# A cross attention's sums over the values kept in one PSUM bank for a whole group of heads, with seven banks in turn and two buffers for an unused output

## The chip, the core and the metric

The kernel runs on one core of a Trainium2 chip. The metric is the device time of one execution in microseconds; the kernel before took 2520.08 (the median of 3 runs, 2517.69 to 2526.74). The engines are named as in the profile: PE is TensorE's matmuls, PEld its weight loads, DVE is VectorE, ACT is ScalarE, POOL is GpSimd and SP is the engine whose queue issues most DMAs.

## What is computed

A small Perceiver network of four layers: 128 rows of width 256 (x) attend to 12544 rows of context, with self attention and feed-forward parts between. Each layer adds three blocks to x: a cross attention (xattn), an attention (attn) and a feed-forward (ffn). The change touches the second cross attention alone:

```python
def _L1_xattn_ref(K_in, V_in, Q_in, mask_attn, mask_pad, Wk, bk, Wv, bv, Wq, bq, Wo, bo):
    # D = 256, NH = 16 heads, DK = 16
    K = (K_in @ Wk + bk).reshape(b, l, NH, DK).transpose(0, 2, 1, 3)
    V = (V_in @ Wv + bv).reshape(b, l, NH, DK).transpose(0, 2, 1, 3)
    Q = (Q_in @ Wq + bq).reshape(b, lp, NH, DK).transpose(0, 2, 1, 3)
    KQ = jnp.einsum('bhld,bhpd->bhlp', K, Q) / np.float32(np.sqrt(DK))
    KQ = KQ + mask_pad.reshape(b, 1, l, 1)
    KQ = KQ + mask_attn.T.reshape(1, 1, l, lp)
    alpha = jax.nn.softmax(KQ, axis=2)
    O = jnp.einsum('bhlp,bhld->bhpd', alpha, V)
    O = O.transpose(0, 2, 1, 3).reshape(b, lp, NH * DK)
    return O @ Wo + bo
```

Here l is 12544, lp is 128, and mask_attn is a matrix of 128 x 12544 that is added to the scores of every head.

## The kernel before

**Stages.** The twelve blocks run one after the other (`run`, L1301). All four cross attentions are one function, `cross` (L361); the second is called as "l1x" with `side=True` (L1317). `side` means that the score has a matrix to be added, which is read from memory in two orders: as it is (`ft`, fetched in `fetch_k`, L441 to 444) and transposed (`gt`, in `fetch_v`, L459 to 464).

**Projections as jobs.** The keys and values of all four cross attentions (`project`, L192) stand in one list of small jobs: a job projects 512 keys (`keys`, L204) or 256 rows of values (`values` of `project`, L220), has ACT or DVE copy the result out of PSUM, and writes it to memory from POOL's queue. `pump` (L142) takes the next jobs of the list. Cross attentions and other blocks pump jobs between their own steps, so a stage also does the projections of later stages. In `cross` a stage's own jobs are due by `goal` (L630 to 633), and others by `rate`, a number per step for each phase: 0.95, 0, 1.2, 1.2 and 0.4 for l1x.

**Steps of cross.** The 12544 context rows are cut into NST = 25 tiles of 512 (the last has 256). The 16 heads are cut into 4 groups (`units`) of 4 (`width`). A step of the loop (L619) handles two things: the scores whose maxima are needed for tile `km`, and, `lead` = 27 steps later, the scores that are exponentiated for tile `ke`. So the first 27 steps have maxima only, the next 73 both, the last 27 only exponentials; at 25 steps a group of heads ends. All is under `manual_schedule` (L616): every engine takes its instructions in the order in which the loop writes them.

Within a step (`scores`, L550), with both:
- set 1: s products of heads 2 and 3, t products of heads 0 and 1, on PE; then their drains;
- set 2: s products of heads 0 and 1, t products of heads 2 and 3; then their drains;
- the jobs that are due (L633, L637);
- `values` (L573): the sums over the values for the tile `ke` of the step before.

An s product (`score_s`, L471) is a matrix of 128 queries x 512 keys in a bank of PSUM. Its drain, with `side`, is one `tensor_tensor_reduce` on DVE (L492): it adds `ft`, takes the maximum into a column of `mxs`, and writes the sum to a tile "junk" that nobody reads; "junk" has one buffer. In the profile it is two instructions, CUSTOM_DVE_ANT_0 and DVE_READ_ACCUMULATOR2_ANT. A t product (`score_t`, L519) is 512 keys x 128 queries in a bank; DVE adds `gt` into the tile `e` (L542) and ACT takes the exponential in place (L547).

`values` multiplies the exponentials with the values (32 matmuls on PE as the profile counts them, tile p, L589) into one bank, and DVE adds that bank to a tile `acc` in SBUF (L595), or copies it there at a group's first tile (L593). After the group `finish` (L597) divides by the sum of the exponentials.

**Banks.** PSUM has eight banks. `bank` (L134) gives out one tile of a whole bank at a time, in turn: bank 1, 2, ... 7, 0. Every user calls it: each head's s and t product, each job, `lower` (L511), `finish` and `values`. A tile of a bank waits until the last reader of the tile that held the bank before is done. PE takes its instructions in order, so a matmul that waits for its bank holds up all that is behind it.

**Loads.** SP's queue issues the loads of keys, values, `ft`, `gt` and context in the loop's order; a load into a buffer that is still being read waits at the head of that queue.

Of the kernel before, what the change touches and what calls it, by code (L numbers as in the profile page):

```python
# [10 lines left out]
F32 = mybir.dt.float32  # L11
# [7 lines left out]
P = 128  # L19
# [6 lines left out]
NST = -(-S2 // ST)  # L26
# [43 lines left out]
def _gelu_kinks():  # L70

    at = [0.25 * i for i in range(17)]
    even = [0.5 * a * math.erf(a / math.sqrt(2.0)) for a in at]
    slope = [(even[i + 1] - even[i]) / 0.25 for i in range(16)]
    return [(at[i], slope[i] - (slope[i - 1] if i else 0.0)) for i in range(16)]


class Net:
    def __init__(self, ctx, tc, io):
        self.tc, self.nc, self.io = tc, tc.nc, io  # L80
        nc = self.nc
        cp = ctx.enter_context(tc.tile_pool(name="const", bufs=1))
        self.small = ctx.enter_context(tc.tile_pool(name="small", bufs=2))
        self.xp = ctx.enter_context(tc.tile_pool(name="x", bufs=2))
        self.wp = ctx.enter_context(tc.tile_pool(name="w", bufs=3))
        self.bp = ctx.enter_context(tc.tile_pool(name="bg", bufs=2))
        self.dp = ctx.enter_context(tc.tile_pool(name="scratch", bufs=1, space=DRAM))
        self.ps1 = ctx.enter_context(tc.tile_pool(name="ps1", bufs=1, space=PSUM))

        self.x = self.xp.tile([P, D], F32, name="x0", tag="x")  # L90
        nc.sync.dma_start(out=self.x, in_=io["x"])
        self.cst = cp.tile([P, NCONST], F32, name="cst", tag="cst")
        nc.sync.dma_start(out=self.cst, in_=io["cst"])
        self.cols = cp.tile([P, NCOL], F32, name="cols", tag="cols")
        nc.scalar.dma_start(out=self.cols, in_=io["cols"])
        self.rows = cp.tile([P, NROW], F32, name="rows", tag="rows")
        nc.gpsimd.dma_start(out=self.rows, in_=io["rows"].to_broadcast([P, NROW]))
        self.eps = {}
        for e in (EPS, 1e-6):
            t = cp.tile([P, 1], F32, name=f"eps{len(self.eps)}", tag=f"eps{len(self.eps)}")  # L100
            nc.vector.memset(t, e)
            self.eps[e] = t
        self.ident = self.const("ident")
        self.kinks = cp.tile([P, 16], F32, name="kinks", tag="kinks")
        for i, (at, _) in enumerate(_gelu_kinks()):
            nc.gpsimd.memset(self.kinks[:, i : i + 1], -at)
        self.fold = cp.tile([P, 64], F32, name="fold", tag="fold")
        nc.gpsimd.tensor_tensor(out=self.fold, in0=self.ident[:, 0:64], in1=self.ident[:, 64:128],
                                op=ALU.add)

        self.plan, self.tiles, self.loaded = [], {}, 0
        self.jobs, self.share, self.credit, self.side = [], 0.0, 0.0, False
        self.turn, self.done = 0, set()

    def const(self, name):
        at, n = CONST_AT[name]
# [17 lines left out]

    def bank(self, name):

        self.turn = (self.turn + 1) % 8
        return self.ps1.tile([P, 512], F32, name=name, tag=f"bank{self.turn}")


# [220 lines left out]
    def cross(self, name, side=False, project=True, rate=()):  # L361
# [2 lines left out]


        nc, tc = self.nc, self.tc
        self.share, self.side = 0.0, side
        width = WIDTH[name]
        units = 16 // width
        lead = NST + 2  # L370
# [2 lines left out]
        with ExitStack() as es:  # L373
# [13 lines left out]
            ps = self.bank(f"{name}_q")  # L387
# [17 lines left out]
            kt, vt, ft, gt, mxs, es_, acc = {}, {}, {}, {}, {}, {}, {}  # L405
# [60 lines left out]
            def tile_of(u, j):  # L466

                at = 32 * ((width * u + j) % 4)
                return slice(at, at + 32)

            def score_s(k, heads):  # L471

                u, i = divmod(k, NST)
                s, m = i * ST, min(ST, S2 - i * ST)
                if u not in mxs:
                    mxs[u] = pool.tile([P, width, NST], F32, name=f"{name}_mxs{u}", tag="mxs",
                                       bufs=2)
                t, at = kt[u, s // SB], s % SB
                banks = {j: self.bank(f"{name}_s{k}_{j}") for j in heads}

                def products():
                    for j in heads:
                        r = tile_of(u, j)
                        nc.tensor.matmul(banks[j][:, :m], qb[u][r, :], t[r, at : at + m],  # L484
                                         start=True, stop=True)

                def drain():
                    for j in heads:
                        if side:
                            junk = ep.tile([P, ST], F32, name=f"{name}_j{k}_{j}", tag="junk",  # L490
                                           bufs=1)
                            nc.vector.tensor_tensor_reduce(  # L492
                                out=junk[:, :m], in0=banks[j][:, :m], in1=ft[k][:, :m], scale=1.0,
                                scalar=-3.0e38, op0=ALU.add, op1=ALU.max,
                                accum_out=mxs[u][:, j, i : i + 1])
                        else:
                            nc.vector.tensor_reduce(out=mxs[u][:, j, i : i + 1],  # L497
                                                    in_=banks[j][:, :m], axis=AX.X, op=ALU.max)
                return products, drain
# [73 lines left out]
            def values(ks):  # L573


                u, i = divmod(ks[0], NST)
                ps = self.bank(f"{name}_p{ks[0]}")
                todo = []
                for k in ks:
                    s = (k - u * NST) * ST  # L580
                    m = min(ST, S2 - s)
                    v, at, e = vt[u, s // SB], (s % SB) // P, es_.pop(k)
                    for a in range(m // P):
                        for j in range(width):
                            c = 17 * (width * (at + a) + j)
                            todo.append(((width * a + j) % 4, v[:, c : c + 32],
                                         e[:, j, a * P : (a + 1) * P]))
                for n, (c, lhs, rhs) in enumerate(todo):
                    nc.tensor.matmul(ps[32 * c : 32 * c + 32, :P], lhs, rhs, start=n < 4,  # L589
                                     stop=n >= len(todo) - 4, skip_group_check=True)  # L590
                if i == 0:
                    acc[u] = self.small.tile([P, P], F32, name=f"{name}_at{u}", tag="at")
                    nc.vector.tensor_copy(acc[u], ps[:, :P])  # L593
                else:
                    nc.vector.tensor_tensor(out=acc[u], in0=acc[u], in1=ps[:, :P], op=ALU.add)  # L595
# [20 lines left out]
            with tc.manual_schedule():  # L616
                for k in (0, 1):
                    fetch_k(k)
                for at in range(total + lead + 3):  # L619
# [21 lines left out]
                    while waiting:  # L641
                        u, i = divmod(waiting[0], NST)
                        n = NST - i if NST - i < 2 * batch else batch
                        last = waiting[0] + n - 1
                        if ke is not None and ke - last < behind - batch + 1:
                            break
                        if last > waiting[-1]:
                            break
                        values(waiting[:n])
                        waiting = waiting[n:]  # L650
                    if ke is not None:
                        waiting.append(ke)
                    u, i = divmod(at - lead - 2 - NST, NST)
# [1 line left out]
                        finish(u)  # L655

            nc.vector.tensor_tensor(out=o, in0=o, in1=self.row(f"{name}_vb"), op=ALU.add)
            self.share, self.side = 1.0, False
            if not project:
                self.add_to_x([o], name)  # L660
                return
# [1 line left out]
            ps = self.one(f"{name}_pr")  # L663
# [720 lines left out]
def _device_arrays(I):  # L1384
# [15 lines left out]
    def cross(name, q, k, v, o=None):  # L1400
        a[f"w_{name}"] = cat(*(_padded(q.T).T,) if o is None else (_padded(q.T).T, o))
        a[f"w_{name}_kv"] = cat(k, v)

    cross("l0x", I["L0_xattn_q_w"].T, I["L0_xattn_k_w"].T, I["L0_xattn_v_w"].T)
    cross("l1x", *(I[f"L1_xattn_W{k}"] for k in "qkvo"))
    cross("l2x", *(I[f"L2_xattn_w{k}"] for k in "qkvo"))
    cross("l3x", *(I[f"L3_xattn_W{k}"] for k in "qkvo"))
    a["w_l0a"] = cat(I["L0_attn_Wq"].T, I["L0_attn_Wk"].T, I["L0_attn_Wv"].T)
# [73 lines left out]
```

## Time and profile before

| | us |
|---|---|
| median of 3 runs | 2520.08 |
| the profiled execution, its own time | 2514.97 |
| its span, first to last instruction | 2513.2 |
| second cross attention, first normalisation to the last sum | about 682 to 1345 |
| PE / DVE / ACT busy between 682 and 1345 | 649.72 / 535.87 / 317.67 |
| L492, the maxima of l1x, x400, busy on DVE | 271.1 |
| L542, the additions of l1x, x400, busy on DVE | 249.9 |
| L595, the additions to `acc`, x96, median of one | 0.280 |
| L593, the copies to `acc`, x4, median of one | 0.290 |

A group's mean is over the full tiles and the shorter last ones. Busy time of PE counts a matmul until its modelled end, and a matmul that stands before a waiting one can be counted as busy while it waits, so starts say more than busy shares. In a line of the timeline the columns are the start, the length, the engine, the line of the kernel, the operation, the output and the inputs; "x8" are eight merged instructions; a bracket gives idle time just before and what ended it.

### The profile page before, as it was taken

Reading aid. Unit: us, or ns where it says so; the run is one execution under the profiler, and the core shown is the slowest. Engines: PE = TensorE matmul, PEld = TensorE weight load, DVE = VectorE, ACT = ScalarE, POOL = GpSimd, SP = SyncE. Lnnn points to the kernel's source line nnn. Section 1 sums busy time; section 2 is a strip of 40 time slices with the busy share of each in tenths; the row PEclk is TensorE's granted clock in tenths of the full one; section 3 lists DMA queues with packets and bytes.
Section 4 is the critical chain, followed back from the end, with each engine's and each line's share of the span. In section 5 each row is a group of like instructions: output and inputs, shape, how many; then the busy total and the mean of one; then the engine's idle time right before and its main releaser. Section 6 shows DMA issues by size and latency. Waiting matters only on the chain.

```text
span 2513.2 us, 76921 instructions
## 1 busy us (share of the span) xinstructions
PE 2344.3 (93%) x32103; PEld 1722.2 (69%) x32103; DVE 1627.1 (65%) x3503; ACT 1144.7 (46%) x2109; POOL 637.6 (25%) x1297
## 2 busy tenths in 40 slices
PE   6989999997899999999999978899999949999969
PEld 3348888874536886666778734468888836888848
DVE  2446688722186788888887721598883579888431
ACT  1212356772213444545584134226668321666842
POOL 6874100015562112444301244630000112000001
PEclk9989999998999999999999989899999978999979
DMA  7768653227788887877665646663332633333216
GB/s 252 217 209 273 200 151 93 78 73 230 255 244 277 275 254 220 241 225 232 215 219 203 197 144 197 194 206 95 91 100 59 211 118 113 94 95 99 65 48 220
DMA packets 200504, 438.90 MB, mean 175 GB/s; under 512 B 33292, under 2 KB 90848, under 8 KB 196064
## 3 DMA queue, kind: packets, MB, share of 16 engines
q1 hardware_dynamic: 148208, 271.33, 35.8%
q0 software_dynamic: 51584, 161.42, 20.0%
q8 instruction: 255, 4.18, 0.7%
q10 hardware_dynamic: 368, 1.25, 0.1%
q14 instruction: 89, 0.73, 0.1%
HBM read 327.69 MB, written 112.58 MB: 175 GB/s over the span
## 4 chain that ended last, share of the span: by engine, by line
PE 33%; issue 14%; DVE 3%; DMA 2%; ACT 1%; POOL 0%; SPq 0%; ACTq 0%; DVEq 0%; POOLq 0%
PE l3x_t L534 5%; PE l3x_p L589 4%; PE l3x_s L484 4%; PE l2x_v L321 3%; PE l3x_k L321 3%; PE l3x_v L321 3%; PE l1x_t L534 2%; PE l1x_p L589 1%; PE l2x_s L484 1%; PE l1f_h L321 1%; PE l1f_o L321 1%; ACT l1x_e L547 1%; PE l2x_k L321 1%; PE l3f_h L321 1%; PE l3f_o L321 1%
## 5 line engine op out<-in xcount | busy, mean ns | idle before, releaser
L547 ACT ACTIVATE l1x_e<-l1x_e 128x512 f32<-128x512 f32 (+1 forms) x400 | 240.6, 622 | 245.9 <-DVE l1x_e L542 245.9
L492 DVE CUSTOM_DVE_ANT_0 l1x_j<-l1x_s,l1x_f 128x512 f32<-128x512 f32 (+1 forms) x400 | 271.1, 678 | 80.6 <-PE l1x_t L534 30.0
L497 DVE TENSOR_REDUCE l0x_mxs<-l0x_s 128x1 f32<-128x512 f32 (+1 forms) x400 | 244.4, 672 | 120.4 <-PE l0x_s L484 89.3
L547 ACT ACTIVATE l0x_e<-l0x_t 128x512 f32<-128x512 f32 (+1 forms) x400 | 203.4, 595 | 176.4 <-PE l0x_t L534 172.9
L547 ACT ACTIVATE l3x_e<-l3x_t 128x512 f32<-128x512 f32 (+1 forms) x400 | 203.4, 595 | 155.6 <-PE l3x_t L534 152.0
L497 DVE TENSOR_REDUCE l2x_mxs<-l2x_s 128x1 f32<-128x512 f32 (+1 forms) x400 | 243.5, 671 | 29.5 <-PE l2x_t L534 23.9
L497 DVE TENSOR_REDUCE l3x_mxs<-l3x_s 128x1 f32<-128x512 f32 (+1 forms) x400 | 242.8, 670 | 27.0 <-PE l3x_t L534 23.9
L547 ACT ACTIVATE l2x_e<-l2x_t 128x512 f32<-128x512 f32 (+1 forms) x400 | 203.5, 595 | 119.4 <-PE l2x_t L534 115.8
L542 DVE TENSOR_TENSOR l1x_e<-l1x_t,l1x_g 128x512 f32<-128x512 f32 (+1 forms) x400 | 249.9, 671 | 11.4 <-PE l1x_t L534 9.1
L534 PE MATMUL l1x_t<-l1x_qb,l1x_kt 32*128 32x128 f32 x3136 | 202.9, 283 | 2.8 <-ACT l1x_vs L238 0.6
L484 PE MATMUL l0x_s<-l0x_kt,l0x_qb 32*128 32x512 f32 (+1 forms) x800 | 190.9, 618 | 15.1 <-ACT l0x_ks L213 9.5
L484 PE MATMUL l1x_s<-l1x_kt,l1x_qb 32*128 32x512 f32 (+1 forms) x800 | 204.2, 616 | 0.6 <-issue 0.5
L484 PE MATMUL l3x_s<-l3x_kt,l3x_qb 32*128 32x512 f32 (+1 forms) x800 | 199.2, 655 | 0.5 <-issue 0.5
L534 PEld LDWEIGHTS l1x_t<-l1x_qb,l1x_kt 32*128 32x128 f32 x3136 | 170.4, 186 | 37.9 <-ACT l2x_ks L213 19.9
L484 PE MATMUL l2x_s<-l2x_kt,l2x_qb 32*128 32x512 f32 (+1 forms) x800 | 184.9, 611 | 0.5 <-issue 0.5
L534 PE MATMUL l3x_t<-l3x_qb,l3x_kt 32*128 32x128 f32 x3136 | 180.5, 280 | 0.1
L534 PE MATMUL l2x_t<-l2x_qb,l2x_kt 32*128 32x128 f32 x3136 | 180.2, 280 | 0.0
L534 PE MATMUL l0x_t<-l0x_qb,l0x_kt 32*128 32x128 f32 x3136 | 179.7, 280 | 0.4 <-DVE l0x_vs L240 0.3
L217 POOL DMA_DIRECT2D l1x_kx<-l1x_ks x208 | 99.5, 486 | 298.9 <-ACT l1x_ks L213 268.1
L534 PEld LDWEIGHTS l3x_t<-l3x_qb,l3x_kt 32*128 32x128 f32 x3136 | 160.3, 186 | 6.8 <-issue 5.0
L534 PEld LDWEIGHTS l0x_t<-l0x_qb,l0x_kt 32*128 32x128 f32 x3136 | 159.4, 186 | 7.3 <-issue 5.0
L534 PEld LDWEIGHTS l2x_t<-l2x_qb,l2x_kt 32*128 32x128 f32 x3136 | 159.9, 186 | 6.2 <-issue 5.0
(606 smaller groups left out, 4050.5 us busy)
## 6 DMA issues: line engine op xcount, KB each, us to landing
l1x_f<-in_fside SPq DMA_DIRECT2D x96, 256.0 KB
l1x_g<-in_fsideT SPq DMA_DIRECT2D x96, 256.0 KB
w<-in_w_l3f POOLq DMA_DIRECT2D x16, 1024.0 KB, 5.1
l0x_kt<-l0x_kx SPq DMA_DIRECT2D x192, 72.0 KB
l1x_kt<-l1x_kx SPq DMA_DIRECT2D x192, 72.0 KB
l2x_kt<-l2x_kx SPq DMA_DIRECT2D x192, 72.0 KB
l3x_kt<-l3x_kx SPq DMA_DIRECT2D x192, 72.0 KB
l0x_vx<-l0x_vs POOLq DMA_DIRECT2D x24, 544.0 KB, 6.6
```

The lines of the kernel that those rows point to most:

```text
L217: nc.gpsimd.dma_start(out=kx[8 * half + h, 2:18, :], in_=t["k"][16 * h : 16 * h + 16, :n])
L321: self.nc.tensor.matmul(out, a, b, start=(i == 0), stop=(i == len(lhs) - 1))
L484: nc.tensor.matmul(banks[j][:, :m], qb[u][r, :], t[r, at : at + m], start=True, stop=True)
L492: nc.vector.tensor_tensor_reduce(out=junk[:, :m], in0=banks[j][:, :m], in1=ft[k][:, :m], scale=1.0, scalar=-3.0e38, op0=ALU.add, op1=ALU.m ...
L497: nc.vector.tensor_reduce(out=mxs[u][:, j, i : i + 1], in_=banks[j][:, :m], axis=AX.X, op=ALU.max)
L534: nc.tensor.matmul(banks[j][:, a * P : (a + 1) * P], t[r, at + a * P : at + (a + 1) * P], qb[u][r, :], start=True, stop=True)
L542: nc.vector.tensor_tensor(out=e[:, j, :m], in0=src, in1=gt[k][:, : m // P, :].rearrange("p a q -> p (a q)"), op=ALU.add)
L547: nc.scalar.activation(e[:, j, :m], src, AF.Exp)
L589: nc.tensor.matmul(ps[32 * c : 32 * c + 32, :P], lhs, rhs, start=n < 4, stop=n >= len(todo) - 4, skip_group_check=True)
```

## The change

For the calls with `side`, which is l1x alone, three things change. `values` no longer takes a bank of the rotation: a group of four heads has one tile of bank 7 for all of its 25 tiles of 512 rows, the matmuls of the later tiles add to what is there, and the bank is copied to `acc` once, after the group's last tile. The rotation goes over seven banks (0 to 6) from the start of the call to its end, and over eight again after it. And "junk" has two buffers. The diff, cut to its core:

```diff
-        self.turn, self.done = 0, set()
+        self.turn, self.ring, self.done = 0, 8, set()
...
     def bank(self, name):

-        self.turn = (self.turn + 1) % 8
+        self.turn = (self.turn + 1) % self.ring
         return self.ps1.tile([P, 512], F32, name=name, tag=f"bank{self.turn}")
...
-        self.share, self.side = 0.0, side
+        self.share, self.side, self.ring = 0.0, side, 7 if side else 8
...
                             junk = ep.tile([P, ST], F32, name=f"{name}_j{k}_{j}", tag="junk",
-                                           bufs=1)
+                                           bufs=2)
...
                 u, i = divmod(ks[0], NST)
-                ps = self.bank(f"{name}_p{ks[0]}")
+                if not side:
+                    ps = self.bank(f"{name}_p{ks[0]}")
+                elif i == 0:
+                    ps = self.ps1.tile([P, 512], F32, name=f"{name}_p{u}", tag="bank7")
+                    acc[u] = ps
+                else:
+                    ps = acc[u]
...
                 for n, (c, lhs, rhs) in enumerate(todo):
-                    nc.tensor.matmul(ps[32 * c : 32 * c + 32, :P], lhs, rhs, start=n < 4,
-                                     stop=n >= len(todo) - 4, skip_group_check=True)
-                if i == 0:
+                    nc.tensor.matmul(ps[32 * c : 32 * c + 32, :P], lhs, rhs,
+                                     start=n < 4 and (i == 0 or not side),
+                                     stop=n >= len(todo) - 4 and (ks[-1] == NST * (u + 1) - 1 or not side),
+                                     skip_group_check=True)
+                if side:
+                    if ks[-1] == NST * (u + 1) - 1:
+                        acc[u] = self.small.tile([P, P], F32, name=f"{name}_at{u}", tag="at")
+                        nc.vector.tensor_copy(acc[u], ps[:, :P])
+                elif i == 0:
                     acc[u] = self.small.tile([P, P], F32, name=f"{name}_at{u}", tag="at")
                     nc.vector.tensor_copy(acc[u], ps[:, :P])
                 else:
...
-            self.share, self.side = 1.0, False
+            self.share, self.side, self.ring = 1.0, False, 8
```

## The prediction

> **What bounds the kernel now.** I first read the engines' shares on the page, then the table of windows over the second attention (cross "l1x", the only one with side=True, so the only code that the change touches), then the timelines of TensorE (PE) and VectorE (DVE) inside it.
>
> ```profile
> PE 2344.3 (93%) x32103; PEld 1722.2 (69%) x32103; DVE 1627.1 (65%) x3503; ACT 1144.7 (46%) x2109; POOL 637.6 (25%) x1297
> ...
> 689.00:751.00 62.00, 61.71 (x220) 24.02 (x220) 49.98 (x145) 10.78 (x16) 43.18 (x83) 1.00 0.81 245
> ...
> 806.50:918.40 111.90, 111.90 (x1416) 94.11 (x1412) 86.27 (x208) 53.83 (x96) 15.46 (x32) 1.00 0.85 270
> 918.40:954.00 35.60, 34.99 (x504) 26.31 (x500) 32.80 (x88) 16.01 (x28) 3.78 (x7) 1.00 0.75 225
> 954.00:1253.00 299.00, 297.42 (x3678) 193.35 (x3678) 254.48 (x639) 149.63 (x252) 113.27 (x237) 0.99 0.76 230
> ```
>
> Columns: window, its length, then busy time of PE, PEld, DVE, ACT and POOL, the granted clock, DMA share, GB/s. PE looks full everywhere, but its ends are modelled, so who waits must be read from starts. DVE is at 81% in the first stretch (only maxima) and 92% in 918 to 954.
>
> ```profile
> 700.41 0.69 DVE L492 CUSTOM_DVE_ANT_0 l1x_j<-l1x_s,l1x_f 128x512 f32<-128x512 f32 x1
> 701.03 0.08 DVE L492 DVE_READ_ACCUMULATOR2_ANT l1x_mxs<- 128x1 f32 x1
> 701.26 0.69 DVE L492 CUSTOM_DVE_ANT_0 l1x_j<-l1x_s,l1x_f 128x512 f32<-128x512 f32 x1
> ...
> 928.50 0.69 DVE L492 CUSTOM_DVE_ANT_0 l1x_j<-l1x_s,l1x_f 128x512 f32<-128x512 f32 x1
> 929.12 0.08 DVE L492 DVE_READ_ACCUMULATOR2_ANT l1x_mxs<- 128x1 f32 x1
> 929.12 1.28 DVE L542 TENSOR_TENSOR l1x_e<-l1x_t,l1x_g 128x512 f32<-128x512 f32 x2
> 930.32 0.28 DVE L595 TENSOR_TENSOR l1x_at<-l1x_at,l1x_p 128x128 f32<-128x128 f32 x1
> 930.51 0.68 DVE L492 CUSTOM_DVE_ANT_0 l1x_j<-l1x_s,l1x_f 128x512 f32<-128x512 f32 x1
> ```
>
> Two things are to be seen. A maximum is followed by the next maximum after 0.84 or 0.85 us, but by an addition after 0.62: the second maximum writes the same "junk" tile and starts 0.14 after the first's accumulator read ends, the addition does not. And the sum l1x_at (L595) takes DVE 0.19 to 0.20 (930.32 to 930.51) in every step. A step in which DVE never idles is 5.50 (925.02 to 930.52 or so, repeated).
>
> Where PE is the slower one, steps of one kind alternate:
>
> ```profile
> 806.52 0.70 PE L484 MATMUL l1x_s<-l1x_kt,l1x_qb 32*128 32x512 f32 x2
> ...
> 807.60 0.61 PE L534 MATMUL l1x_t<-l1x_qb,l1x_kt 32*128 32x128 f32 x8
> ...
> 808.49 3.72 PE L321 MATMUL l1x_v<-l1x_kvw,l1x_cv 128*128 128x256 f32 x16
> 812.14 1.08 PE L589 MATMUL l1x_p<-l1x_e,l1x_vt 128*32 128x128 f32 x32
> 813.15 0.70 PE L484 MATMUL l1x_s<-l1x_kt,l1x_qb 32*128 32x512 f32 x2
> ...
> 814.31 0.69 DVE L492 CUSTOM_DVE_ANT_0 l1x_j<-l1x_s,l1x_f 128x512 f32<-128x512 f32 x1 [0.73 <-PE l1x_t L534]
> 814.93 0.08 DVE L492 DVE_READ_ACCUMULATOR2_ANT l1x_mxs<- 128x1 f32 x1
> ```
>
> The step from 806.52 lasts 6.63: first set 1.01, second set 0.96, two projections 3.65, values 1.01. The second set's t products begin 1.08 after the step. The next step (813.15 to 820.50) lasts 7.35, because its t products had to wait for their bank until 1.60. DVE's first maximum starts 1.16 after the step's start, as soon as its score is there.
>
> **Bank waits, by counting.** A step takes banks in the order s2 s3 t0 t1 | s0 s1 t2 t3 | projections (n of them) | p. With eight banks a tile waits for the one eight places back; before, t2 so waits for the last projection of the step before (or t3 where n is 0), and t3 for the p of the step before. The waits agree:
>
> ```profile
> PEld l1x_t L534 <- ACT l2x_ks L213: 19.9, 30, 0.9
> ```
>
> After, p leaves the rotation, and the ring is seven. Counting seven back, every tile of a step up to t2 waits for the same predecessor as before (n = 0, 1 and 2). Three differ: t3 now waits for **s2 of the same step**, the first projection for s3 and the second for t0 of the same step.
>
> **The change part by part.**
>
> 1. Sums in PSUM. It removes 96 additions (L595) of 0.20 on DVE. The 4 copies (L593, 0.29) move to a group's end, where a group's next p, a step later, waits for them: DVE has done them by then, so zero; uncovered it would be 4 x 0.3 = 1.2 us. The matmuls are the same. Their own bank wait goes: on PE, p starts at the end of the projections already (812.14 is 808.49 + 3.65), so nothing is won there.
>
> 2. Two junk tiles. Each maximum that follows a maximum starts 0.22 to 0.23 earlier (0.84 becomes 0.61). A full step on DVE falls from 5.50 by 0.20 + 2 x 0.22 to 4.86; a step of four maxima alone from 3.36 to some 2.5.
>
> 3. Seven banks. Where DVE waits for PE at a step's start, the first maximum ends at 1.16 + 0.70, and the semaphore reaches PE 0.06 later (at 930.40 an addition ended, at 930.46 PE went on). So t3 cannot start before 1.92, in every step that has both products. In order behind it on PE: the rest of the set, projections, p, the next step. From a late t3 to the end of the set it took 1.07 (t3 free at 930.66, p at 931.73); the projections start at 2.99, against 1.97 in an unhindered step and 2.69 (820.50 less 4.66) in the hindered one. From there to the step's end the rows show 2.93 for n = 1 (1228.97: 2.57 to 5.50) and 4.66 for n = 2. So a step becomes 5.92 (n = 1) and 7.65 (n = 2). DVE's 4.86 fits inside, and DVE meanwhile has three other drains, so it does not starve. If the part of t2 issued earlier shortens the tail to 0.88 (814.96 to 815.84), they are 5.73 and 7.46.
>
> **The sum, stretch by stretch.**
> - 689 to 751, maxima alone: 18 steps of 3.36 on DVE. PE's floor is 2.99 (718.20 to 721.19: four scores and one projection of keys). 18 x 0.37 = 6.7, less the 1.5 of two stalls there that are not DVE's: -5.2 at most. DMA at 81% would go to some 90%; I take -5. The 5.5 us wait for a context block at 751 and the PE-bound steps to 806 stay.
> - 806.5 to 918.4: 16 steps with n = 2, 111.8 in all, 6.99 each. 16 x 7.65 = 122.4: **+10.6** (+7.5 with the short tail).
> - 918.4 to 954: one step n = 1 that goes from 4.91 to 5.92, then six without projections, which DVE bounds: five to six times 0.64 less, the first lost to the longer step: -2.5.
> - 954 to 1253: 31 steps n = 1 outside the group changes, 181.0 in all, become 31 x 5.92 = 183.5: +2.5. Eight steps n = 2, 7.30 on average, become 7.65: +2.8. (Short tail: -3.4 and +1.3.) The steps at the two group changes are taken as they are.
> - 1253 to 1345, no maxima: the chain there is t, four additions, four exponentials, p; the sum comes after the additions and hides behind PE, so 0 (at best -1 or -2).
>
> Total: -5 + 10.6 - 2.5 + 2.5 + 2.8 = **+8.4 us**; bounds -2 and +15. On the profiled span of 2513.2 (2514.97 with what lies around it) that is 2521.6. The profiled run lies 5 below the median of 2520.08; put on the median the forecast is 2528, +0.3%, which is within 0.5% (12.6 us), about what a measurement of this kernel can tell from no change.
>
> [...]
>
> **Rivals.**
> - **A, the wait is hidden (faster).** If t3's new predecessor does not hold PE up (another order of banks than I counted, or s2 drained earlier), what remains is DVE's relief. n = 1 steps go to 4.9 (1.97 + 2.93): 31 x 4.9 - 181 = -29; n = 2 to 6.63: -5.7 in the third stretch and 8 x 0.6 = -5 later; with -5 and -2.5 this is -47: 2473. For it: DVE is at 85% in 954 to 1253 and the waits for ACT there come from DVE being late. Against: the same counting gives before's waits. Chance 0.16, most of it with a part of that gain, about 2500.
> - **B, the pause between maxima is not the tile's (slower).** If it belongs to the accumulator read that each maximum ends with, the second buffer wins nothing: the first stretch stays, the fourth gives back 1 instead of 2.5, and the sum is 10.6 + 5.3 - 1 = +15 to +16: 2536. It decides as soon as a maximum after a maximum still takes over 0.8. For it: only maxima carry that read. Against: the addition after the read does not pause. Chance 0.20.
> - **C, DMA bounds the first stretch (slower).** 81% and 245 GB/s now; 751 to 760 shows 96% at 299. If each step still takes 3.3, the sum is +13.4: 2533. Chance 0.10.
> - **Forecast** 0.54: of it 0.42 within 0.5%, 0.12 above (its bound of +15 lies over 12.6).
>
> So faster 0.16, same 0.42, slower 0.20 + 0.10 + 0.12 = 0.42. The forecast's own range is 2518 to 2535. The range for 8 in 10 takes in B and C with the medians' spread (2517.69 to 2526.74), and A's milder part: 2508 to 2542.
>
> **What will show it.** Maxima 0.61 apart in the first stretch, its steps near 3.0 (else B or C). In 806 to 918, equal steps of about 7.5 to 7.65 in place of 6.63 and 7.35, with PEld l1x_t waiting for DVE l1x_mxs from 1.1 to 1.9 after each step's start; if that wait is absent or the steps are 6.63, A. Steps near 4.9 at 930. No L595 rows, four copies at the groups' ends. A wait of p for a copy of over 1 us, or a stall at the start of the next stage, would be something I have not counted.

## The result, and the profile after

The changed kernel takes 2516.97 us (median of 12 runs, 2503.3 to 2527.15), the kernel before 2518.24 in the 12 runs beside them. The ratio is 1.0002, 95% interval 0.9984 to 1.002: no change that can be measured. The profiled execution of the changed kernel has a span of 2515.0 against 2513.2. The second attention alone, from its first score to its last sum over values, went from 651.5 to 649.9 us in the two profiles.

That the total stands still hides much movement. First the busy time of the changed kernel's engines:

```profile
PE 2347.4 (93%) x32103; PEld 1723.6 (69%) x32103; DVE 1586.1 (63%) x3407; ACT 1144.3 (45%) x2109; POOL 638.6 (25%) x1297
```

DVE has 96 instructions and 41 us less, PE is nearly as it was. The windows of the second attention, in the columns used above:

```profile
688.00:742.00 54.00, 53.38 (x204) 19.96 (x203) 41.48 (x132) 10.03 (x15) 34.82 (x68) 0.94 0.83 257
...
797.30:919.90 122.60, 122.60 (x1417) 95.03 (x1410) 78.86 (x192) 54.77 (x97) 15.50 (x32) 1.00 0.79 249
919.90:953.20 33.30, 32.72 (x502) 25.09 (x499) 31.04 (x82) 15.96 (x28) 3.79 (x7) 1.00 0.79 235
953.20:1251.40 298.20, 298.00 (x3681) 198.22 (x3677) 236.82 (x593) 149.63 (x253) 113.38 (x237) 1.00 0.76 230
```

The stretch with two projections per step was 111.9 long and is 122.6; PE counts as busy through all of it, in both. Where the time went is seen in the starts. PE's timeline of one such step:

```profile
805.01 0.70 PE L484 MATMUL l1x_s<-l1x_kt,l1x_qb 32*128 32x512 f32 x2
805.03 0.71 PE L534 MATMUL l1x_t<-l1x_qb,l1x_kt 32*128 32x128 f32 x8
805.55 0.59 PE L484 MATMUL l1x_s<-l1x_kt,l1x_qb 32*128 32x512 f32 x2
805.58 0.67 PE L534 MATMUL l1x_t<-l1x_qb,l1x_kt 32*128 32x128 f32 x9
806.02 0.60 PE L484 MATMUL l1x_s<-l1x_kt,l1x_qb 32*128 32x512 f32 x2
806.09 0.27 PE L534 MATMUL l1x_t<-l1x_qb,l1x_kt 32*128 32x128 f32 x1
806.46 0.59 PE L484 MATMUL l1x_s<-l1x_kt,l1x_qb 32*128 32x512 f32 x2
806.93 1.15 PE L534 MATMUL l1x_t<-l1x_qb,l1x_kt 32*128 32x128 f32 x14
808.01 3.72 PE L321 MATMUL l1x_v<-l1x_kvw,l1x_cv 128*128 128x256 f32 x16
811.66 1.08 PE L595 MATMUL l1x_p<-l1x_e,l1x_vt 128*32 128x128 f32 x32
812.67 0.70 PE L484 MATMUL l1x_s<-l1x_kt,l1x_qb 32*128 32x512 f32 x2
```

Of the second set's 16 t matmuls two go by 806.09, both of t2; the other 14 wait until 806.93, which is 1.92 after the step's start, and the step lasts 7.66. All 16 steps of the stretch are alike; the alternation of 6.63 and 7.35 is gone. DVE in the same step, then PEld's waits for t products in this stretch (total, times, longest), first in the changed kernel, then in the kernel before:

```profile
806.17 0.69 DVE L492 CUSTOM_DVE_ANT_0 l1x_j<-l1x_s,l1x_f 128x512 f32<-128x512 f32 x1 [2.73 <-PE l1x_t L534]
806.79 0.08 DVE L492 DVE_READ_ACCUMULATOR2_ANT l1x_mxs<- 128x1 f32 x1
806.79 0.69 DVE L492 CUSTOM_DVE_ANT_0 l1x_j<-l1x_s,l1x_f 128x512 f32<-128x512 f32 x1
```

```profile
PEld l1x_t L534 <- DVE l1x_mxs L492: 11.3, 16, 0.7
...
PEld l1x_t L534 <- ACT l1x_vs L238: 1.6, 8, 0.2
```

The first maximum's read ends at 806.87, and PE goes on at 806.93. Sixteen such waits in sixteen steps; before, PEld l1x_t waited here eight times for ACT's copy of a projection and never for a maximum. The second maximum starts at 806.79, 0.62 after the first: the pause of 0.14 behind the read is gone. The first stretch shows the same, 0.61 to 0.62 from one maximum to the next:

```profile
701.23 0.69 DVE L492 CUSTOM_DVE_ANT_0 l1x_j<-l1x_s,l1x_f 128x512 f32<-128x512 f32 x1
701.84 0.08 DVE L492 DVE_READ_ACCUMULATOR2_ANT l1x_mxs<- 128x1 f32 x1
701.84 0.69 DVE L492 CUSTOM_DVE_ANT_0 l1x_j<-l1x_s,l1x_f 128x512 f32<-128x512 f32 x1
```

### The profile page after: what moved, and what is told of

Its sections match the earlier page's. It is cut to its first block, busy times and chain, and to the rows that moved or that the text cites. A ratio compares the mean times of both kernels' runs of the same rounds, so it can differ in the third digit from the quotient of the medians.

```text
span 2515.0 us, 76743 instructions
## 1 busy us (share of the span) xinstructions
PE 2347.4 (93%) x32103; PEld 1723.6 (69%) x32103; DVE 1586.1 (63%) x3407; ACT 1144.3 (45%) x2109; POOL 638.6 (25%) x1297
## 3 DMA queue, kind: packets, MB, share of 16 engines
q1 hardware_dynamic: 148208, 271.33, 35.4%
## 4 chain that ended last, share of the span: by engine, by line
PE 31%; issue 13%; DVE 3%; DMA 2%; ACT 2%; POOL 0%; DVEq 0%; ACTq 0%; POOLq 0%
PE l3x_t L534 5%; PE l3x_p L595 4%; PE l3x_s L484 4%; PE l3x_k L321 3%; PE l3x_v L321 3%; PE l2x_v L321 2%; PE l2x_s L484 1%; ACT l1x_e L547 1%; PE l3f_h L321 1%; PE l3f_o L321 1%; PE l1f_h L321 1%; PE l1f_o L321 1%; DMA l1x_g<-in_fsideT 1%; PE l1x_t L534 0%; PE l1x_p L595 0%
## 5 line engine op out<-in xcount | busy, mean ns | idle before, releaser
L492 DVE CUSTOM_DVE_ANT_0 l1x_j<-l1x_s,l1x_f 128x512 f32<-128x512 f32 (+1 forms) x400 | 253.0, 676 | 135.4 <-PE l1x_t L534 104.8
L534 PE MATMUL l1x_t<-l1x_qb,l1x_kt 32*128 32x128 f32 x3136 | 222.4, 285 | 1.4 <-DVE l1x_mxs L492 0.6
L534 PEld LDWEIGHTS l1x_t<-l1x_qb,l1x_kt 32*128 32x128 f32 x3136 | 182.8, 186 | 46.3 <-DVE l1x_mxs L492 27.5
L484 PE MATMUL l0x_s<-l0x_kt,l0x_qb 32*128 32x512 f32 (+1 forms) x800 | 193.0, 617 | 17.9 <-ACT l0x_ks L213 11.5
L484 PE MATMUL l1x_s<-l1x_kt,l1x_qb 32*128 32x512 f32 (+1 forms) x800 | 186.7, 621 | 0.8 <-issue 0.5
```

The costliest lines, as they stand in the source:

```text
L492: nc.vector.tensor_tensor_reduce(out=junk[:, :m], in0=banks[j][:, :m], in1=ft[k][:, :m], scale=1.0, scalar=-3.0e38, op0=ALU.add, op1=ALU.m ...
L534: nc.tensor.matmul(banks[j][:, a * P : (a + 1) * P], t[r, at + a * P : at + (a + 1) * P], qb[u][r, :], start=True, stop=True)
```

## The experiments

All runs compute the whole network. Lengths of steps are differences of starts on PE's timeline, as above. Each column of the table is one profiled execution ("projections between" is the edit further down, on the changed kernel). The table cuts the second attention at the first score, the first t product, the end of its own last value projection, the first key projection of the third attention, the last score and the last p.

| us from one cut to the next | before | changed | junk alone | banks alone | projections between |
|---|---|---|---|---|---|
| maxima alone | 103.6 | 94.3 | 95.0 | 105.2 | 100.5 |
| mostly two projections per step | 129.5 | 140.5 | 125.1 | 140.9 | 124.8 |
| none | 35.4 | 31.5 | 32.2 | 36.4 | 31.0 |
| one or two | 291.5 | 291.0 | 278.7 | 293.1 | 269.4 |
| exponentials alone | 91.5 | 92.6 | 91.3 | 91.7 | 89.5 |
| all | 651.5 | 649.9 | 622.3 | 667.2 | 615.2 |

The first row scatters by several us between executions of one and the same kernel: the run "junk alone" was made twice and shows 95.0 and 97.6 there, "projections between" 100.5 and 96.6. The second row came out the same both times (125.1; 124.8), the fourth within 1.3 (278.7 and 278.4; 269.4 and 270.7).

**The parts apart: the second junk tile alone.**

```diff
 # on the kernel before
-                                           bufs=1)
+                                           bufs=2)
```

> The kernel before with two junk tiles and nothing else (eight banks in turn, sums added by VectorE). My theory, that the pause between maxima is a wait for the junk tile: maxima 0.61 apart, steps of the first stretch 2.99 in place of 3.36, 9 to 10 us less there; the stretch with two projections per step keeps its alternation of 6.63 and 7.35; steps without projections fall from 5.50 to 5.06 (-2.6 in all); steps with one projection come in pairs whose sum falls from 11.86 to 11.42 (0.22 a step, -7 to -8 in all). In all -20 us, ratio 0.992. Rival, that the pause goes only together with the other parts, or that it is hidden outside the first stretch: 0 or -10, ratio 1.000 or 0.996.

Measured: 2484.67, ratio 0.9885 (0.985 to 0.9921); a second series on another occasion, below, 0.9909 (0.9888 to 0.993). The maxima of a step with two projections:

```profile
808.48 0.69 DVE L492 CUSTOM_DVE_ANT_0 l1x_j<-l1x_s,l1x_f 128x512 f32<-128x512 f32 x1 [0.73 <-PE l1x_t L534]
809.09 0.08 DVE L492 DVE_READ_ACCUMULATOR2_ANT l1x_mxs<- 128x1 f32 x1
809.09 0.69 DVE L492 CUSTOM_DVE_ANT_0 l1x_j<-l1x_s,l1x_f 128x512 f32<-128x512 f32 x1
```

The steps are those expected: pairs such as 5.03 + 6.36 and 5.51 + 5.89, with sums of 11.3 to 11.5; 5.03 without projections. It won more than the -20 expected (-29 in the span). The hindered steps with two projections also fell, from 7.35 to 6.89, which I had put at nothing: the exponentials end earlier, so the copy of the projection, which stands behind them on ACT, frees t2's bank earlier (in the step from 807.32 it ends at 808.40, 1.08 after the start, and t2 follows at 808.45; before, in the step from 813.15, at 814.69, 1.54 after it, and 814.75).

**The seven banks and the sums in PSUM, without the second junk tile.**

```diff
 # on the changed kernel
-                                           bufs=2)
+                                           bufs=1)
```

> The changed kernel with one junk tile (seven banks, sums in a bank of their own). My theory, that the seventh place back holds t3 up until the first maximum of its own step: steps of 7.66 (two projections) and 5.92 (one) as in the changed kernel, 5.30 without projections, the first stretch as before the change (3.36 a step). In all +8 to +12 us against the kernel before, ratio 1.003 to 1.005. Rival, that the parts hardly matter each by itself: ratio 1.000 and steps of 6.63 and 7.35.

Measured: 2529.17, ratio 1.0046 (1.0026 to 1.0067); steps of 7.66 and 5.92 to 5.94, 3.36 in the first stretch. One step with two projections, from its start to the next one's:

```profile
823.21 0.70 PE L484 MATMUL l1x_s<-l1x_kt,l1x_qb 32*128 32x512 f32 x2
...
825.12 1.15 PE L534 MATMUL l1x_t<-l1x_qb,l1x_kt 32*128 32x128 f32 x14
...
830.87 0.70 PE L484 MATMUL l1x_s<-l1x_kt,l1x_qb 32*128 32x512 f32 x2
```

So the change is a gain of about 1% and a loss in one. What the junk tile wins depends on the banks: 0.9885 with eight, and 1.0002/1.0046 = 0.996 with seven, where the handshake between PE and DVE, not DVE's load, sets the steps.

**Which part of the banks: the ring, or the accumulating?**

```diff
 # on the kernel before, with the ring of seven and bufs=2 as in the change
+                if side:
+                    ps = self.ps1.tile([P, 512], F32, name=f"{name}_p{ks[0]}", tag="bank7")
+                else:
                     ps = self.bank(f"{name}_p{ks[0]}")
```

> Seven banks in turn, two junk tiles, the sums in bank 7, but begun anew and added by VectorE for every tile of 512 rows, as before the change. My theory (it is the count of the banks that holds t3 up): steps of 7.66 and 5.92 as in the changed kernel, and 5.06 in place of 4.83 without projections; 1 to 3 us more than the changed kernel. Rival (that it is the accumulating in one bank over a whole group that makes the equal, longer steps): steps of 6.6 to 7.35 with two projections.

One execution: span 2527.6. The steps with two projections, again on PE:

```profile
823.98 0.70 PE L484 MATMUL l1x_s<-l1x_kt,l1x_qb 32*128 32x512 f32 x2
...
825.89 1.15 PE L534 MATMUL l1x_t<-l1x_qb,l1x_kt 32*128 32x128 f32 x14
826.98 3.72 PE L321 MATMUL l1x_v<-l1x_kvw,l1x_cv 128*128 128x256 f32 x16
830.63 1.08 PE L592 MATMUL l1x_p<-l1x_e,l1x_vt 128*32 128x128 f32 x32
831.64 0.70 PE L484 MATMUL l1x_s<-l1x_kt,l1x_qb 32*128 32x512 f32 x2
```

The same 1.91 and 7.66, with 5.92 and 5.03 to 5.04 in the other steps: it is the ring. Accumulating costs PE nothing: with it the steps are the same 7.66 and 5.92. The second attention is 3.8 longer than in the changed kernel: 1.1 where there are no projections, 4.1 in the first stretch, which scatters, and 1.5 less in the last. The span's other 9 us lie outside the second attention, which the edit does not touch, in a single execution.

**One bank fewer.**

```diff
 # on the changed kernel
-        self.share, self.side, self.ring = 0.0, side, 7 if side else 8
+        self.share, self.side, self.ring = 0.0, side, 6 if side else 8
```

> The changed kernel with six banks in turn in place of seven (one bank is left unused). My theory: t2 now waits for s2 of its step and t3 for s3, whose maximum ends 0.61 later, so steps of 8.27 (two projections) and 6.53 (one), the first stretch unchanged; some 60 steps x 0.61 = +37 us against the changed kernel. Rival (t3 starts late for another reason, such as its weight load or a busy row group): the steps stay at 7.66 and 5.92.

One execution: span 2563.7, 48.7 above the changed kernel. PE and DVE in one step:

```profile
818.67 0.70 PE L484 MATMUL l1x_s<-l1x_kt,l1x_qb 32*128 32x512 f32 x2
...
820.59 1.76 PE L534 MATMUL l1x_t<-l1x_qb,l1x_kt 32*128 32x128 f32 x16
822.28 3.72 PE L321 MATMUL l1x_v<-l1x_kvw,l1x_cv 128*128 128x256 f32 x16
825.93 1.08 PE L595 MATMUL l1x_p<-l1x_e,l1x_vt 128*32 128x128 f32 x32
826.94 0.70 PE L484 MATMUL l1x_s<-l1x_kt,l1x_qb 32*128 32x512 f32 x2
```

```profile
819.83 0.69 DVE L492 CUSTOM_DVE_ANT_0 l1x_j<-l1x_s,l1x_f 128x512 f32<-128x512 f32 x1 [3.34 <-PE l1x_t L534]
820.45 0.09 DVE L492 DVE_READ_ACCUMULATOR2_ANT l1x_mxs<- 128x1 f32 x1
820.45 0.69 DVE L492 CUSTOM_DVE_ANT_0 l1x_j<-l1x_s,l1x_f 128x512 f32<-128x512 f32 x1
821.06 0.08 DVE L492 DVE_READ_ACCUMULATOR2_ANT l1x_mxs<- 128x1 f32 x1
```

Now t2 starts when the first maximum is done (820.54) and t3 when the second is (821.14); the set's end moves by 0.61 and the step to 8.27, and to 6.53 with one projection, both as expected. The count of the banks gives the length of these steps to 0.01 us. The three stretches with both products grew by 39.8 in all (11.1, 1.0 and 27.7), against +37 expected; the first stretch was 7.9 longer and the last 1.7, in a single execution.

**Giving PE work while the first maximum runs.** The projections need nothing of the step's scores. They are moved between the sets, on the changed kernel and on the kernel before with two junk tiles.

```diff
-                for part in sets:
+                for i, part in enumerate(sets):
+                    if i == 1:
+                        between()
                     parts = [make(k, heads) for make, k, heads in part]
...
+                if len(sets) == 1:
+                    between()
...
-                    scores(ke, km)
+                    def work(at=at):
+                        nonlocal due
                         left = sum(1 for (n, _, _), _ in self.jobs if n == name)
...
+                    scores(ke, km, work if side else lambda: None)
```

> The changed kernel with the projections that are due in a step issued between its two sets in place of after them (the second attention only; the same projections in the same steps). My theory: TensorE then has 1.9 or 3.65 us of work while VectorE takes the first maximum, t2 and t3 find their banks free, and a step is 1.01 + 0.97 + 1.01 plus the projections: 6.64 with two, 4.9 with one (VectorE's 4.86 is then the bound). Some 24 x 1.0 + 37 x 1.0 = -50 to -60 us, ratio 0.977 to 0.98. Rival: another wait takes its place (VectorE without scores while the projections run, ScalarE's copies, loads at 280 GB/s), and the steps with one projection stay over 5.5: ratio 0.99 or more.

> The kernel before with two junk tiles and the projections between the sets: eight banks in turn, sums added by VectorE. My theory: t3 waits for s2 of its own step here too, but the projections cover it; VectorE bounds steps with one projection at 5.06 or so, two projections take 6.64. Ratio 0.98 to 0.985, some 8 us more than the changed kernel with the same edit, which is then what the sums in PSUM are worth. Rival: with eight banks it is as fast as with seven or faster, so the sums in PSUM win nothing.

Measured: 0.9847 (0.9815 to 0.9878) on the changed kernel and 0.9849 (0.9821 to 0.9878) on the one before. The changed kernel's step with this edit:

```profile
827.42 0.70 PE L484 MATMUL l1x_s<-l1x_kt,l1x_qb 32*128 32x512 f32 x2
...
828.52 3.72 PE L321 MATMUL l1x_v<-l1x_kvw,l1x_cv 128*128 128x256 f32 x16
832.17 0.70 PE L484 MATMUL l1x_s<-l1x_kt,l1x_qb 32*128 32x512 f32 x2
832.19 0.71 PE L534 MATMUL l1x_t<-l1x_qb,l1x_kt 32*128 32x128 f32 x8
...
833.28 1.08 PE L600 MATMUL l1x_p<-l1x_e,l1x_vt 128*32 128x128 f32 x32
834.29 0.70 PE L484 MATMUL l1x_s<-l1x_kt,l1x_qb 32*128 32x512 f32 x2
```

The wait is gone: the second set begins at 832.17, right after the projections, and its t products 0.02 later. The step is 6.87, not the 6.64 expected, and 5.13 or 5.25 with one projection, not 4.9: two sets that follow each other take 1.01 + 0.97, two that are parted 1.10 + 1.11. Why parted sets take longer no run here shows. This seam of 0.23 a step, and up to 0.35 where there is one projection, is by my estimate some 15 us over the 60 steps, most of what is missing from the 50 to 60 us expected. And with the wait covered, seven banks with the sums in PSUM and eight with the sums on DVE do equally well: the rival of the second of these runs holds, and no ratio here shows a gain from keeping the sums in PSUM.

**The seam tried: the values between the sets too.**

```diff
                             due -= 1.0
+                        if side:
+                            sums()
```

(`sums` is the loop over `waiting` that calls `values`, which after the step is then run only without `side`.)

> The changed kernel with the projections and the sums over the values (p) between the two sets, so that a step's second set and the next step's first set follow each other on TensorE. My theory: two sets that follow each other overlap at their seam (2.0 in place of 1.10 + 1.10), so 6.63 with two projections and 4.9 with one, where the edit with the projections alone between showed 6.87 and 5.16: 10 to 15 us less than that, ratio 0.979 to 0.981. Rival: the next step's first set now comes so soon that its banks (t1 waits for the s0 of the step before) are still being read, and the wait returns there: the steps stay at 5.2 or longer, ratio 0.985 or more.

> The same edit on the kernel before with two junk tiles (eight banks, sums added by VectorE, whose addition now stands between the drains of the two sets and waits for p). My theory: VectorE waits for p in each step, some 0.4, and then for the second set: 5.1 to 5.3 with one projection, 6.63 with two; 5 to 10 us slower than its twin with the sums in PSUM. Rival: no difference between the two.

> The kernel before with two junk tiles once more, beside the two above on the same chip. Expected from its first run: ratio 0.9885 (0.985 to 0.992). If the projections between the sets are worth what their steps show (5.16 against 5.70, 6.87 against 6.76 to 7.0), it is slower by 8 to 15 us than the edits with projections between.

> The changed kernel with the projections alone between the sets once more, beside the others on the same chip. Expected from its first run: ratio 0.985 (0.982 to 0.988).

| run | ratio to the kernel before | median |
|---|---|---|
| seven banks, projections and values between | 1.0054 (1.0032 to 1.0076) | 2527.86 |
| eight banks, two junk tiles, the same edit | 0.9941 (0.9921 to 0.9962) | 2500.94 |
| eight banks, two junk tiles alone, again | 0.9909 (0.9888 to 0.993) | 2491.84 |
| seven banks, projections alone between, again | 0.9851 (0.9829 to 0.9873) | 2475.88 |

The first of these is the miss of the study. Its steps:

```profile
1047.87 0.70 PE L484 MATMUL l1x_s<-l1x_kt,l1x_qb 32*128 32x512 f32 x2
...
1049.33 1.61 PE L534 MATMUL l1x_t<-l1x_qb,l1x_kt 32*128 32x128 f32 x16
1050.87 1.98 PE L321 MATMUL l2x_k<-l2x_ck,l2x_kvw 128*128 128x512 f32 x4
1052.78 1.08 PE L600 MATMUL l1x_p<-l1x_e,l1x_vt 128*32 128x128 f32 x32
1053.79 0.70 PE L484 MATMUL l1x_s<-l1x_kt,l1x_qb 32*128 32x512 f32 x2
```

They are 5.92 and 7.66 again, to the hundredth. With all other work between the sets, the second set of a step and the first of the next follow each other, and that pair is eight tiles in a ring of seven just as the old pair was; its last tile (t1) waits for its first (s0):

```profile
1049.03 0.69 DVE L492 CUSTOM_DVE_ANT_0 l1x_j<-l1x_s,l1x_f 128x512 f32<-128x512 f32 x1 [0.99 <-PE l1x_t L534]
1049.65 0.08 DVE L492 DVE_READ_ACCUMULATOR2_ANT l1x_mxs<- 128x1 f32 x1
```

The read ends at 1049.73, and the weight loads for t1, which waited for it, go on at 1049.78, 1.91 after the pair's start at 1047.87. I had named this wait in the rival and not counted it in the forecast. With eight banks the pair fits, and there the same edit is faster than with seven, the opposite of what I expected of it; but DVE waits for p between the drains (1.15 in a step at 1043.48), the steps are 5.38 and 6.02, and it loses to the plain junk edit.

The best found is the changed kernel with the projections between the sets: 0.9847 and 0.9851 in two series, 16 us faster than the junk tile alone on the same chip (2475.88 against 2491.84). In the kernel before, the projections between do as well.

## Why the prediction was right

The forecast was 2528, within 0.5%; measured 2517, no change. The mechanisms of both large parts were right, and their sizes in the steps. The sum behind the forecast, +8.4, was not: it lies above the measured interval, which is -4 to +5 us (0.9984 to 1.002). 2517 is just under the forecast's own range of 2518 to 2535. By its steps:

- **Seven banks.** Right in mechanism and size. t3 starts 1.92 after the step's start (predicted 1.92), projections 3.00 (2.99), steps 7.66 and 5.92 (7.65 and 5.92). The long tail, not the short one, was the true one. The third stretch grew by 10.7 (10.6). (One reading was off without effect: before, the second set's t products begin 0.96 after the step and not 1.08; the row at 807.60 starts with the third of them.) That the ring is the cause is shown by the runs with six banks and with the ring alone.
- **Two junk tiles.** Right: 0.61 between maxima, steps of 4.83 without projections (4.86), first-stretch steps of 2.98 (2.99), -2.25 in the fourth stretch (-2.5). What I had not worked out is what this part is worth by itself, 0.9 to 1.2%: in the steps with both products the ring hides most of it.
- **Sums in PSUM.** The additions went; the copies at the groups' ends cost nothing that shows.
- **The sum.** +8.4 was forecast, the second attention shows -1.6 (the profiled spans +1.8). Three terms were mis-sized and one was missing:
  - "The 5.5 us wait for a context block at 751 ... stay": it was 1.5, and the way to 806 was 10.0 shorter, not 5; the steps up to the wait gave 3.9 of that and the wait itself 4.0. The latter is chance and no work of the change as far as these runs show: in two executions of the kernel with the junk tile alone the same wait is 3.8 and 6.6.
  - "31 steps n = 1 ..., 181.0 in all": PE's starts before give 183.4 for the 31 full steps with one projection outside the group changes, so +0.1 was to be expected of them and not +2.5. The 32 such steps, one of them short, grew by 0.3 together. The eight with two projections grew by 2.2 (2.8).
  - "The steps at the two group changes are taken as they are": the steps around them, 954 to 969 and 1093 to 1125, were 1.7 and 2.0 shorter. Of the second, 1.4 is a fall of the clock in the one execution before (below).
  - The last stretch, taken as 0, grew by 1.1.

  Without the wait and the clock the second attention would show some +4 (an estimate: -1.6 + 4.0 + 1.4), inside the measured interval. These are pieces of a size that single executions scatter by: two executions of one kernel differ in the second attention by 2.6 and 2.8 (projections between: 615.2 and 612.6; junk alone: 622.3 and 625.1).
- **Rival A** fell: the wait is there in every such step. **B** fell: the pause went with the second tile, which takes 0.23 off every maximum that follows a maximum and, alone, 0.9 to 1.2% off the kernel. Where the junk tile need not be waited for, the rows show the next maximum 0.61 after the start of one that lasts 0.69. **C** fell: 2.98 per step at 257 GB/s.

## What to carry to other kernels

When a ring of buffers is shortened, count places back for every tile of a step: it matters less how many tiles are in use than whether one comes to wait for a tile of its own step, which ties producer and consumer together however fast the consumer has become: here the steps with two projections took 7.66 us with one junk tile and with two. A scratch output that nobody reads can still cost time if the same instruction writes it twice in a row; here a second buffer won 0.23 us a pair. And where two edits go together, time each alone: here one of them won 0.9 to 1.2% by itself, and the other, put on top of it, took that back.

## What the hardware showed that I had not expected

The granted clock falls to about half for some us in a stage where PE counts as nearly always busy. In the kernel before, at a group change, and in the changed kernel at its first value projection:

```profile
1118.60:1122.00 3.40, 3.40 (x10) 1.62 (x7) 3.13 (x8) 1.91 (x4) 0.00 (x0) 0.51 0.05 13
...
748.80:752.20 3.40, 3.40 (x8) 2.31 (x8) 0.83 (x4) 0.00 (x0) 2.67 (x6) 0.50 1.02 277
```

(The last three columns are the clock, the DMA share and GB/s.) The step at the group change lasted 10.77. Its two projections took 5.08 from their start to p (1118.96 to 1124.04); the same two take 3.63 in the changed kernel (1117.40 to 1121.03), so some 1.4 of the step goes with the clock. PE's weight loads had waited 0.55 and 0.94 for banks in the four us before the fall. The one in the changed kernel follows PE's wait of 1.5 for a context block, which ended at 748.68. In the kernel before, where that wait was 5.5 and ended at 756.46, the clock was 0.50 from 753.3 to 760.1.

In windows of 0.05 us the clock stands at 0.50 from 1118.5 to 1121.9 in the kernel before and from 748.8 to 752.2 in the changed one, 3.4 us each; the stretch from 753.3 to 760.1 is twice as long, 6.8. What brings a dip about, after waits as short as 0.55, 0.94 and 1.5 us, is not shown by these runs.

And two maxima in a row that write the same elements of one tile are 0.84 apart instead of 0.61, although nobody reads the tile in between.
